# Where the first pair's row terms come from in the opening of a two-layer graph attention kernel, and the order of the work around it

## The chip, the cores and the metric

The kernel runs on one core of a Trainium2 chip. The metric is the device time of one execution in microseconds (us), and the number that counts is the median of several runs. The engines are PE (TensorE, matrix products; PEld is its loading of the stationary operand), DVE (VectorE), ACT (ScalarE), POOL (GpSimd) and SP (SyncE, which here issues the DMAs). Each engine works through a queue of its own in order; semaphores let one wait for another.

## The reference

Two layers over the same graph of 4096 nodes with 256 features: first a network of two graph attention (GAT) steps, then a transformer block whose attention is masked by the same adjacency matrix. Only the first GAT step matters here.

```python
def _gat_layer(x, adj_mat, W, a):            # H = 8 heads, O = 32
    Wh = jnp.einsum('nd,hdo->hno', x, W)
    src = jnp.einsum('hno,ho->hn', Wh, a[:, :O])
    dst = jnp.einsum('hno,ho->hn', Wh, a[:, O:])
    e = jax.nn.leaky_relu(src[:, :, None] + dst[:, None, :], LRELU_SLOPE)
    e = jnp.where(adj_mat[None, :, :] > 0, e, NEG_INF)
    alpha = jax.nn.softmax(e, axis=-1)
    out = jnp.einsum('hnm,hmo->hno', alpha, Wh)
    return jnp.transpose(out, (1, 0, 2)).reshape(N, -1)

h = jax.nn.elu(_gat_layer(x, adj_mat, W1, a1)) + x
out = jax.nn.elu(_gat_layer(h, adj_mat, W2, a2)) + h     # then the transformer
```

`adj` is a 4096 x 4096 matrix of int32.

## The kernel before

**How attention is computed.** exp(leaky_relu(src + dst)) is one of two products of a row factor and a column factor, according to the sign of src + dst. So the kernel builds no exponentials of pairs. For each tile of 128 columns it keeps values that are already multiplied by the two column factors (`vst`, as two fp16 halves), and one-byte matrices that say for each pair whether it is an edge (`mask`) and whether its sum lies on the upper side (`t8`). PE multiplies them (L1462) and adds up in six PSUM banks.

**Groups.** The work of both GAT steps is a list of 256 groups `(l, nb, p, g)`: step, block of 1024 rows, pair of heads, and quarter of 512 columns ("quarter" below means one of these eight pieces, as the change's name does). Eight groups make up one pair of heads for one block. For group i the list `compare(i)` makes `t8`: for each of four column tiles k and two heads j it compares the row terms `s_b` with the column's term `negd` (on DVE as a tensor_scalar, L1124, or on ACT as a Sign, L1122) and then ands the result with the mask on DVE (L1137). `s_b` holds the row terms of a pair of heads, repeated in all 128 partitions; `s_fetch` (L1090) reads it from `s_d` in memory, two DMAs of 512 KB.

**What else the first groups carry.** Quarters are prepared by `preparation(l, q, ...)`: 512 rows of x are transposed on PE (`features`, L991, copied by ACT, L1000); for each of four tiles PE makes the values and terms (`values_out`, L1005, f32), ACT takes exponentials and copies the terms (L1018 to L1020), DVE takes a maximum (L1023) and multiplies by the factors (L1036, L1045) into `prod`; `split` writes the first fp16 half on ACT (L1051) or DVE (L1053) and the second on POOL (L1054). `prod` lies in `ev_broad` for quarter 0 and in `g_prod`, with two buffers, for quarter 1. At last `term_rows` turns a quarter's row terms on PE (L1059), copies them on ACT into `g_sr`, which has one buffer (L1065), and writes them to `s_d` with four small DMAs (L1068).

The adjacency matrix is loaded in units of 256 rows by 512 columns (L858, 512 KB each, buffers `g_adj`, of which there are three; the first eight units have five places elsewhere as well). A unit is clipped to one byte by DVE (`mask_clip`, L867), which also asks for the next load; it is turned on PE (L892) and put into the mask by ACT (L898), and every second one is stored to memory. Four units make the mask of one quarter.

**Order.** In `begin` (L1288) the queues of PE, ACT, DVE and SP follow the written order; after it those of PE, ACT and DVE do, and the steps of preparation, compares, turns and clips are put between the products of each group by due times (`side`). Group i carries `compare(i + 2)`, so `begin` makes `compare(0)` and `compare(1)`. It also prepares quarters 0 and 1 and clips and turns the eight units of their masks; group 0 starts on quarter 2, whose units are in `turns[0]`, the list `ahead`. A few small loads of later code may be put between the DMAs of `begin`.

Written order of `begin` before: loads; features of both quarters; the weights' terms (`weights_steps`); values of quarter 0, with two clips; its term rows; values of quarter 1 with the splits of both and two more clips; its term rows; `s_fetch`; four turns with four clips; `compare(0)`; four turns with the four clips of `ahead`; `compare(1)`.

Of the kernel before, what the change touches and what calls it, by code (L numbers as in the profile page):

```python
# [8 lines left out]
F32 = mybir.dt.float32  # L9
# [13 lines left out]
P = 128  # L23
# [728 lines left out]
def graph_attention(  # L752
# [27 lines left out]
    nc = tc.nc  # L780
    N = adj.shape[0]
    H, D, O = weights[0][0].shape
    DC = D // P
# [4 lines left out]
    W = BT * P  # L788
# [26 lines left out]
    def turn_bank(shape, dtype):  # L815
        return ps.tile(shape, dtype, name="turn", tag="turn", bufs=2)

    spare = []

    def spare_bank():  # L820

        spare.append(0)
        return ps.tile([P, 512], F32, name=f"bank{(len(spare) - 1) % 6}")

# [148 lines left out]
    def rows_ahead(l, q, width=D):  # L975
        if q < NG:
            r = coming_rows[l, q] = rows_p.tile([P, G, D], F32, name="g_rows")
            rows[l].load(r[:, :, :width], G * q, slice(0, width))

    def preparation(l, q, bank, first=False):  # L980
# [32 lines left out]
        def values_in(t):  # L1013
            at = G * q + t
            pv = held.pop(("v", t))
            big = some.tile([P, 2, H], F32, name="g_big", bufs=4)
            for i, scale in enumerate((-1.0, -LRELU)):
                nc.scalar.activation(big[:, i, :], pv[:, D + H : D + 2 * H], AF.Exp, scale=scale)  # L1018
            nc.scalar.activation(L.r[:, at, :], pv[:, D : D + H], AF.Exp, scale=LRELU - 1.0)
            nc.scalar.copy(  # L1020
                L.terms[:, :, at, :], pv[:, D : D + 2 * H].rearrange("p (k h) -> p k h", k=2)
            )
            nc.vector.tensor_reduce(  # L1023
                L.tops[:, at : at + 1], pv[:, :D], AX.X, ALU.max, apply_absolute_value=True
            )

            if l == 0 and q != 1:
                if t == 0:
                    held["prods"] = ep.tile([P, G, H, 2, V1], F32, name="ev_broad")
                prod = held[t] = held["prods"][:, t]  # L1030
            elif l > 0 and t % 2 == 0:
                prod = held[t] = rows_p.tile([P, H, 2, V1], F32, name="g_adj", bufs=3)
            else:
                prod = held[t] = some.tile([P, H, 2, V1], F32, name="g_prod")
            by_head = big.rearrange("p i h -> p h i").unsqueeze(3)
            nc.vector.tensor_tensor(  # L1036
                prod[:, :, :, :O],
                pv[:, :D].rearrange("p (h o) -> p h o", o=O).unsqueeze(2).to_broadcast([P, H, 2, O]),
                by_head.to_broadcast([P, H, 2, O]),
                op=ALU.mult,  # L1040
            )
            if l > 0:
                nc.scalar.mul(prod[:, :, :, O:], by_head, UP)
            else:
                nc.vector.tensor_scalar(prod[:, :, :, O:], by_head, UP, None, op0=ALU.mult)  # L1045
# [41 lines left out]
    def take(n):  # L1087
        return [step for _ in range(min(n, len(later))) for step in later.pop(0)]

    def s_fetch(l, nb, p):  # L1090
        s_b = s_p.tile([P, 2, W], F32, name="s_b")
        first, n = STARTS[l][nb] * P, TILES[l][nb] * P
        for j in range(2):
            row = s_d[l][2 * p + j : 2 * p + j + 1, first : first + n]
            nc.sync.dma_start(s_b[:, j, :n], spread(row, [[0, P], [1, n]]))
        return s_b
# [6 lines left out]
    def compare(i):  # L1103

        l, nb, p, g = groups[i]
        L, s_b = layers[l], s_of[l, nb, p]
        t8 = s8[i] = t_p.tile([P, 2, NW, G, HB], F8, name="t8")
        more = (7, 11, 15, 23, 27, 31)
        if l > 0 or (nb + 1 == len(TILES[l]) and p + 1 < H // 2):
            more = (3, 7, 11, 15, 19, 23, 27)  # L1110
        if apart(i):
            u8[i] = [rows_p.tile([P, NW, G, HB], F8, name="g_adj", bufs=3) for j in range(2)]

        def step(k):
            mt = g * G + k
            for j in range(2):
                to = t8[:, j, :, k, :]
                s = s_b[:, j, :].rearrange("p (w n) -> p w n", n=HB)
                negd = L.negd[:, mt, 2 * p + j : 2 * p + j + 1]

                if (j == 1 or mt in more) and not (i == 0 and k == 0):
                    nc.scalar.activation(to.bitcast(I8), s, AF.Sign, bias=negd, scale=-1.0)  # L1122
                else:
                    nc.vector.tensor_scalar(  # L1124
                        to, s, negd, -1.0, op0=ALU.is_ge, op1=ALU.mult, saturate=False
                    )

        def mask():
            both = t8.rearrange("p j w g n -> p j (w g n)").bitcast(I32)
            m32 = masks[l, nb][g].rearrange("p w g n -> p (w g n)").bitcast(I32)  # L1130
            for j, u in enumerate(u8.get(i, ())):
                nc.vector.scalar_tensor_tensor(
                    u.rearrange("p w g n -> p (w g n)").bitcast(I32),
                    t8[:, j].rearrange("p w g n -> p (w g n)").bitcast(I32),
                    -1, m32, op0=ALU.bitwise_xor, op1=ALU.bitwise_and,
                )
            nc.vector.scalar_tensor_tensor(  # L1137
                both, m32.unsqueeze(1).to_broadcast(list(both.shape)), SIGNS, both,
                op0=ALU.bitwise_or, op1=ALU.bitwise_and,
            )  # L1140

        return [lambda k=k: step(k) for k in range(G)] + [mask]

    def pair_end(l, nb, p, ev):
# [127 lines left out]
    def load_ahead(n):  # L1272
        for _ in range(min(n, len(coming))):
            mask_load(*coming.pop(0))
# [13 lines left out]
    def begin():  # L1288
# [15 lines left out]
        def clip(k):  # L1304
            mask_clip(*units[k], load=False)
# [4 lines left out]
        def both(use):  # L1310
            use[0]()
            use[1]()

        (f_0, v_0, part_0, row_0), (f_1, v_1, part_1, row_1) = (
            preparation(0, q, spare_bank, True) for q in range(2)
        )
        for use in f_0 + f_1:
            both(use)
        for step in weights_steps(0):
            step()  # L1320
        for use in v_0[:2]:
            both(use)
        for k in range(2):
            clip(k)
            both(v_0[2 + k])
        both(row_0)
        for k in range(4):
            both(v_1[k])
            part_0[k]()
            if k < 2:  # L1330
                clip(2 + k)
            if k > 1:
                part_1[k - 2]()
        both(row_1)
        s_of[0, 0, 0] = s_fetch(0, 0, 0)
        rows_ahead(0, 2)
        for k in range(4):
            turn(k)
            if k < 2:
                part_1[2 + k]()  # L1340
            clip(4 + k)
        load_ahead(3)
        ahead = turns[0]
        for step in compare(0):
            step()
        for k in range(4, len(units)):
            turn(k)
            mask_clip(*ahead[k - 4])
        for step in compare(1):
            step()  # L1350

    ev = acc = None
    ordered = {mybir.EngineType.PE, mybir.EngineType.Activation, mybir.EngineType.DVE}
# [821 lines left out]
```

## Time and profile before

| | us |
|---|---|
| median of 3 runs | 3158.15 |
| lowest and highest | 3156.18, 3162.9 |
| the profiled execution's own time | 3161.47 |
| its span | 3159.7 |
| PE busy | 3084.4 (98%) |
| DVE busy | 2786.5 (88%) |
| ACT busy | 2682.1 (85%) |
| POOL busy | 1196.6 (38%) |

The opening, in stretches of 10 us (busy time of each engine):

| stretch | PE | DVE | ACT | granted PE clock | GB/s |
|---|---|---|---|---|---|
| 0 to 10 | 1.85 | 4.16 | 2.18 | 1.00 | 204 |
| 10 to 20 | 9.49 | 7.31 | 6.22 | 1.00 | 383 |
| 20 to 30 | 2.77 | 8.51 | 5.50 | 0.77 | 116 |
| 40 to 50 | 6.76 | 6.05 | 7.62 | 0.88 | 282 |
| 50 to 60 | 8.18 | 9.64 | 6.23 | 0.83 | 265 |
| 70 to 80 | 9.48 | 9.48 | 8.17 | 1.00 | 266 |
| 100 to 110 | 9.63 | 9.49 | 7.93 | 1.00 | 200 |
| 120 to 130 | 8.55 | 8.87 | 8.21 | 1.00 | 120 |

A line of the timeline reads: start in us, duration in us, engine, line of the code, operation, what it writes and reads, shapes, how many instructions are merged, and in brackets how long the engine was idle before and what ended that. "bank" and "turn" are PSUM banks, "t" is `t8`, "adj" a clipped unit. A line of the stretches reads: from and to, length, then busy time and instructions of PE, PEld, DVE, ACT and POOL, the granted clock, the DMA share and GB/s. The clock is recorded from 11.7 us on; the 1.00 before that is not a record.

### The profile page before, as it was taken

How to read it: one execution, taken by the hardware profiler on the slowest of the kernel's cores; microseconds unless marked ns; L12 is line 12 of the kernel's file. 1: busy time of each engine (PE TensorE's matmuls, PEld its weight loads, DVE VectorE, ACT ScalarE, POOL GpSimd, SP SyncE). 2: the span in 40 equal slices, each digit the busy share in tenths (PEclk: the TensorE clock that was granted, in tenths of full speed). 3: DMA queues.
4: the chain of work that ended last, by engine and by line, in shares of the span. 5: the costliest groups of instructions: out<-in, count | busy, mean ns of one | idle time of the engine just before them, and what ended most of it. 6: DMA issues, size and time to landing. Idle time of an engine off the chain costs nothing. (4 is left out here: it accounts for less than half of the span.)

```text
span 3159.7 us, 138934 instructions
## 1 busy us (share of the span) xinstructions
PE 3084.4 (98%) x63976; PEld 2715.3 (86%) x63976; DVE 2786.5 (88%) x3140; ACT 2682.1 (85%) x3228; POOL 1196.6 (38%) x538
## 2 busy tenths in 40 slices
PE   6999999999999999999998999999999999999998
PEld 5899999999889999999975888888878888877766
DVE  7999999999889999999976999999999999998221
ACT  6899999999899999999965888888888888886232
POOL 3300000000320000000003988898988888997110
PEclk8999999999999999999999999999999999999999
DMA  7666554420311213121145010101011010121210
GB/s 259 220 201 197 166 190 149 151 86 23 112 44 39 79 56 96 42 67 38 46 127 158 14 41 21 34 21 34 28 27 39 18 49 8 48 61 56 70 34 22
DMA packets 212034, 250.33 MB, mean 79 GB/s; under 512 B 88241, under 2 KB 132785, under 8 KB 211441
## 3 DMA queue, kind: packets, MB, share of 16 engines
q1 hardware_dynamic: 211440, 241.36, 24.9%
q8 instruction: 502, 8.22, 1.1%
q14 instruction: 92, 0.75, 0.1%
HBM read 198.84 MB, written 42.47 MB: 76 GB/s over the span
## 5 line engine op out<-in xcount | busy, mean ns | idle before, releaser
L1462 PE MATMUL bank<-vst,t 128*128 128x132 f16 x16384 | 1457.3, 220 | 9.7 <-DVE t L1137 9.5
L1946 POOL TENSOR_TENSOR u_both<-u_e 128x1024 f32<-128x1024 f32 x448 | 1049.7, 2385 | 902.8 <-DMA u_k<-half_d 782.8
L1462 PE MATMUL bank<-vst,mask 128*128 128x132 f16 (+1 forms) x10516 | 1372.4, 206 | 0.0
L1122 ACT ACTIVATE t<-s_b,g_terms 128x1024 int8<-128x1024 f32 x1234 | 1320.8, 1162 | 24.3 <-PE bank L1462 18.9
L1462 PEld LDWEIGHTS <-t 128*128 128x128 fp8e4 x16384 | 1186.4, 96 | 22.9 <-DVE t L1137 12.5
L1828 DVE SCALAR_TENSOR_TENSOR u_e<-u_mask,u_ps 128x1024 f32<-128x1024 uint8 x1024 | 1165.9, 1220 | 23.7 <-ACT u_ps L1826 20.6
L1826 ACT ACTIVATE u_ps<-u_ps 128x1024 f32<-128x1024 f32 x1024 | 1030.0, 1008 | 147.4 <-PE u_ps L1819 49.4
L1462 PEld LDWEIGHTS <-mask 128*128 128x128 fp8e4 x10516 | 920.7, 98 | 0.0
L1137 DVE SCALAR_TENSOR_TENSOR t<-mask,t 128x2048 int32<-128x2048 int32 x256 | 588.5, 2299 | 74.8 <-ACT t L1122 66.5
L1819 PE MATMUL u_ps<-u_q,u_k 128*32 128x512 f16 x8192 | 642.6, 383 | 11.0 <-issue 7.3
L1837 PE MATMUL u_av<-u_e,u_v 128*32 128x128 f32 x16384 | 605.7, 273 | 2.6 <-issue 2.6
L1837 PEld LDWEIGHTS u_av<-u_e,u_v 128*32 128x32 f32 x16384 | 492.0, 110 | 131.5 <-issue 5.2
L1124 DVE TENSOR_SCALAR t<-s_b,g_terms 128x1024 fp8e4<-128x1024 f32 x814 | 591.0, 758 | 2.4 <-DMA s_b<-s_d 2.4
L1054 POOL TENSOR_TENSOR vst<-g_adj,vst 128x528 f16<-128x528 f32 x16 | 19.8, 1239 | 727.2 <-ACT g_big L1018 682.7
L1837 PE MATMUL u_dn<-u_both,u_ones 128*32 128x128 f32 x7168 | 281.9, 273 | 1.6 <-issue 1.6
L1819 PEld LDWEIGHTS <-u_k 128*32 128x32 f16 x8192 | 231.4, 95 | 58.6 <-issue 17.9
L1837 PEld LDWEIGHTS u_dn<-u_both,u_ones 128*32 128x32 f32 x7168 | 213.7, 110 | 41.9 <-issue 2.1
L2041 ACT ACTIVATE u_hid<-misc,n_b 128x512 f32<-128x512 f32 x64 | 43.9, 687 | 140.2 <-PE misc L2034 140.1
L2054 PE MATMUL misc<-u_k,u_hid 128*128 128x256 f32 x512 | 111.8, 379 | 0.0
L2034 PE MATMUL misc<-ln_cols,u_k 128*128 128x512 f32 x256 | 111.3, 592 | 0.5 <-ACT ln_cols L1558 0.5
L2054 PEld LDWEIGHTS misc<-u_k,u_hid 128*128 128x128 f32 x512 | 96.7, 190 | 13.3 <-issue 0.5
L2034 PEld LDWEIGHTS misc<-ln_cols,u_k 128*128 128x128 f32 x256 | 48.6, 190 | 58.5 <-issue 56.9
(171 smaller groups left out, 1808.9 us busy)
## 6 DMA issues: line engine op xcount, KB each, us to landing
g_adj<-in_adj_dram SPq DMA_DIRECT2D x123, 512.0 KB
s_b<-s_d SPq DMA_DIRECT2D x64, 512.0 KB
mask<-mask SPq DMA_DIRECT2D x128, 256.0 KB
u_mask<-mask SPq DMA_DIRECT2D x32, 512.0 KB
mask<-stage SPq DMA_DIRECT2D x48, 256.0 KB
half_d<-u_halves SPq DMA_DIRECT2D x32, 256.0 KB
u_q<-half_d SPq DMA_DIRECT2D x32, 256.0 KB
rows<-e_x SPq DMA_DIRECT2D x31, 256.0 KB
```

Of the source, the lines that this page charges most:

```text
L1122: nc.scalar.activation(to.bitcast(I8), s, AF.Sign, bias=negd, scale=-1.0)
L1124: nc.vector.tensor_scalar(to, s, negd, -1.0, op0=ALU.is_ge, op1=ALU.mult, saturate=False)
L1137: nc.vector.scalar_tensor_tensor(both, m32.unsqueeze(1).to_broadcast(list(both.shape)), SIGNS, both, op0=ALU.bitwise_or, op1=ALU.bitwise_and,)
L1462: nc.tensor.matmul(to, left, right, start=k not in opened, stop=last)
L1819: nc.tensor.matmul(ps[r * O : (r + 1) * O, j, :], k_st[c][:, 2 * u + j, at : at + O], q_st[:, h, :], start=True, stop=True,)
L1826: nc.scalar.activation(ps, ps, AF.Exp, scale=SCALE)
L1828: nc.vector.scalar_tensor_tensor(e, mask, 0.0, ps, op0=ALU.not_equal, op1=ALU.mult)
L1837: nc.tensor.matmul(to[j * O : (j + 1) * O, at], lefts[j], es[j // 2][:, j % 2, at], start=first and part == 0, stop=last and part == PARTS ...
L1946: nc.gpsimd.tensor_tensor(both, es_of[i - 1][u], es_of[i][u], op=ALU.add)
L2034: nc.tensor.matmul(ph, w1_sb[:, k, f * P : (f + 1) * P], hn[:, k, :], start=(k == 0), stop=(k == DC - 1),)
L2041: nc.scalar.activation(hid[:, f, :], ph, AF.Gelu_apprx_tanh, bias=norms.sb["b1"][:, f : f + 1])
L2054: nc.tensor.matmul(po[:, :D], hid[:, f, at : at + P], w2_sb[:, f, :], start=(f == 0), stop=(f == FC - 1),)
```

## The change

The change rewrites the order of `begin` and takes the first pair's row terms for block 0 from PE instead of from memory.

- `s_spread(q, j, bank)` multiplies the features of quarter q by one column of the weights, head j's row term, repeated 128 times as the stationary operand. So all 128 partitions of a bank hold that head's row terms, and ACT copies them into `s_b`. Four calls (two heads, two quarters) fill `s_b` for the first pair; `s_fetch(0, 0, 0)` goes. The term rows are still written to `s_d` for the later pairs, at the end of `begin`.
- Twelve f32 products of the identity with itself are put ahead of the features, in a bank of their own (`bank5`), and read by nobody.
- The values of quarter 1 are made after `compare(0)`; the four clips of `ahead` come after `compare(1)`; the rows of quarter 2 and three loads of adjacency are asked for earlier; turns 4 to 7 and both term rows come behind quarter 1's values.
- `banks_of(order)` names the PSUM bank of each step in place of a round of six; term rows use a "turn" bank.
- For quarters 0 and 1 ACT writes the small part of `prod` (L1045 before).
- `compare(0)` returns its steps head by head, and for groups 0 and 1 the tiles k = 0 and 1 of the second head are compared on DVE (before: only k = 0 of group 0).

```diff
-    spare = []
-
-    def spare_bank():
-
-        spare.append(0)
-        return ps.tile([P, 512], F32, name=f"bank{(len(spare) - 1) % 6}")
+    def banks_of(order):
+
+        left = list(order)
+
+        def bank():
+            k = left.pop(0)
+            if k is None:
+                return turn_bank([P, 512], F32)
+            return ps.tile([P, 512], F32, name=f"bank{k}")
+
+        return bank
...
-            if l > 0:
+            if first or l > 0:
                 nc.scalar.mul(prod[:, :, :, O:], by_head, UP)
...
+    def s_spread(q, j, bank):
+
+        L = layers[0]
+        pt = bank()
+        for c in range(DC):
+            nc.tensor.matmul(
+                pt,
+                L.w_ext[:, c, D + j : D + j + 1].to_broadcast([P, P]),
+                L.ft[q][:, c, :],
+                start=(c == 0),
+                stop=(c == DC - 1),
+            )
+        nc.scalar.copy(s_of[0, 0, 0][:, j, q * HB : (q + 1) * HB], pt)
...
-        def step(k):
+        def step(k, heads=range(2)):
             mt = g * G + k
-            for j in range(2):
+            for j in heads:
...
-                if (j == 1 or mt in more) and not (i == 0 and k == 0):
+                if (j == 1 or mt in more) and not (i < 2 and k < 2):
...
+        if i == 0:
+            return [lambda k=k, j=j: step(k, (j,)) for j in range(2) for k in range(G)] + [mask]
...
-            preparation(0, q, spare_bank, True) for q in range(2)
+            preparation(0, q, banks_of(order), True)
+            for q, order in ((0, (0, 1, 4, 5, 0, 1, None)), (1, (2, 3, 4, 5, 2, 3, None)))
         )
+        warm = ps.tile([P, 512], F32, name="bank5")
+        for _ in range(12):
+            nc.tensor.matmul(warm[:, :P], ident_f, ident_f, start=True, stop=True)
         for use in f_0 + f_1:
             both(use)
         for step in weights_steps(0):
             step()
-        for use in v_0[:2]:
-            both(use)
-        for k in range(2):
-            clip(k)
-            both(v_0[2 + k])
-        both(row_0)
+        rows_ahead(0, 2)
+        clip(0)
         for k in range(4):
-            both(v_1[k])
-            part_0[k]()
-            if k < 2:
-                clip(2 + k)
-            if k > 1:
-                part_1[k - 2]()
-        both(row_1)
-        s_of[0, 0, 0] = s_fetch(0, 0, 0)
-        rows_ahead(0, 2)
+            both(v_0[k])
+            if k > 0:
+                part_0[k - 1]()
+                clip(k)
+        part_0[3]()
+        clip(4)
+        s_of[0, 0, 0] = s_p.tile([P, 2, W], F32, name="s_b")
+        s_bank = banks_of((2, 3, 0, 1))
+        for j in range(2):
+            for q in range(2):
+                s_spread(q, j, s_bank)
+        load_ahead(3)
+        ahead = turns[0]
+        comparing = compare(0)
+        for step in comparing[:G]:
+            step()
         for k in range(4):
             turn(k)
-            if k < 2:
-                part_1[2 + k]()
-            clip(4 + k)
-        load_ahead(3)
-        ahead = turns[0]
-        for step in compare(0):
+        clip(5)
+        for step in comparing[G:]:
             step()
-        for k in range(4, len(units)):
+        for use in v_1:
+            use[0]()
+        for k in range(6, 8):
+            clip(k)
+        for k in range(4):
+            v_1[k][1]()
+            if k > 0:
+                part_1[k - 1]()
+        part_1[3]()
+        for k in range(4, 8):
             turn(k)
-            mask_clip(*ahead[k - 4])
+        both(row_0)
+        both(row_1)
         for step in compare(1):
             step()
+        for u in ahead:
+            mask_clip(*u)
```

## The prediction

> **What bounds the kernel now.** I read four views of the execution before: the page, the stretches of ten microseconds, the timeline engine by engine from 0 to 140 us, and the waits. The page says that TensorE is busy for nearly the whole span; the chain that ended last lies in the transformer and does not reach back to the opening. So the question is only how long the opening takes and what passes its delay on.
>
> ```profile
> PEclk8999999999999999999999999999999999999999
> ...
> 30.00:40.00 10.00, 1.83 (x15) 1.57 (x16) 7.12 (x9) 6.18 (x8) 0.00 (x0) 0.50 0.89 299
> ...
> 60.00:70.00 10.00, 8.96 (x107) 7.62 (x105) 9.48 (x14) 8.02 (x24) 4.59 (x3) 1.00 0.76 244
> ...
> 130.00:140.00 10.00, 10.00 (x193) 10.00 (x191) 9.81 (x17) 10.00 (x15) 2.58 (x1) 1.00 0.70 250
> ```
>
> From 130 us on PE is busy in every microsecond; before that it is not. Between 30 and 40 us it works 1.83 of 10 us, at half clock (0.50). The timeline says what it waited for:
>
> ```profile
> 26.71 0.83 SPq L1095 DMA_DIRECT2D s_b<-s_d  x2
> ...
> 33.63 3.23 ACT L1122 ACTIVATE t<-s_b,g_terms 128x1024 int8<-128x1024 f32 x3 [4.82 <-DMA s_b<-s_d]
> 33.63 2.74 DVE L1124 TENSOR_SCALAR t<-s_b,g_terms 128x1024 fp8e4<-128x1024 f32 x4 [2.14 <-DMA s_b<-s_d]
> 36.89 2.29 DVE L1137 SCALAR_TENSOR_TENSOR t<-mask,t 128x2048 int32<-128x2048 int32 x1 [0.52 <-ACT t L1122]
> 39.24 0.40 PE L1462 MATMUL bank<-vst,t 128*128 128x132 f16 x2 [0.78 <-DVE t L1137]
> ...
> 44.94 0.70 DVE L867 TENSOR_SCALAR adj<-g_adj 128x1024 fp8e4<-128x1024 int32 x1 [3.72 <-DMA g_adj<-in_adj_dram]
> ...
> 47.73 2.29 DVE L1137 SCALAR_TENSOR_TENSOR t<-mask,t 128x2048 int32<-128x2048 int32 x1
> ...
> 50.54 0.42 DVE L1023 TENSOR_REDUCE g_tops<-turn 128x1 f32<-128x256 f32 x1
> 51.61 0.40 PE L892 MATMUL turn<-g_ident_h,adj 128*128 128x128 f16 x4 [3.07 <-DVE ev_broad L1036]
> 61.04 2.29 DVE L1137 SCALAR_TENSOR_TENSOR t<-mask,t 128x2048 int32<-128x2048 int32 x1 [0.52 <-ACT t L1122]
> 74.90 2.29 DVE L1137 SCALAR_TENSOR_TENSOR t<-mask,t 128x2048 int32<-128x2048 int32 x1 [0.52 <-ACT t L1122]
> ```
>
> The terms come back from memory at 33.63, so the first group starts at 39.24. But the start is not what is passed on. Group 0 halts at 48.5 until DVE reaches the third quarter's values at 50.54 (PE's 3.07 us wait), since DVE's queue still holds the opening's tail: the second compare's mask (47.73) and a clip that waited 3.72 us for its adjacency tile. From there every group takes the same time: L1137 stands at 47.73, then 61.04, 74.90, 102.69, 116.55, 130.42, 13.86 us apart, DVE 95 to 100% busy, and after 130 PE is full. Nothing there has slack, so **the end moves by as much as DVE's first values of group 0 (50.54) move**. That is my yardstick, not the start at 39.24.
>
> **The change, part by part.** Times "after" are worked out queue by queue, each in its written order, with pitches (start to start) read from the timeline: a values step 0.34 + 0.60 us on DVE (L1023, L1036), a clip 0.61, a compare 0.67, a mask 2.2, a Sign on ACT 1.07 (3.23 for three), a turn's copy on ACT 0.5.
>
> *Warm matmuls.* Twelve f32 products of 128 columns. The trace has none; L1005's halves of 272 columns take 0.24 us each at clock 1.00, so by columns 24 halves take 2.7 us, twice that at half clock. PE is idle until 8.15 (rows landing) and the identity is made by 1.41: 6.7 us of cover, cost nothing. The sixteen first transposes take 0.24 us each; a block of four took 1.06 at clock 0.50 (39.89) and 0.60 at 1.00 (60.03), so they gain up to 1.6 us. The trace's landings put the quarters' rows at 8.0 and 9.5, which leaves 1.1: the values start at 10.4 instead of 11.52. Bounds 0 and 1.6. The Trainium skill (TensorE: Matmul & The Clock Gate, Part 1: The HAM clock gate) says the same, half rate until about 3.4 us of activity, but also that one idle window takes it back; were the gap between the warm matmuls and the rows such a window, its sum would be 0 of gain.
>
> *First quarter's values with clips 0 to 4.* 4 × 0.94 + 5 × 0.61 = 6.8 us of DVE from 10.9 (landing of the first adjacency tile; one more each 1.36 us): done 18.1. ACT takes over L1045 (0.23 us each, as L1043 does in layer 1).
>
> *Spread by PE.* Eight f32 products of 512 columns. The page's L2034 row has 256 records in 111.3 us for 128 such products, 0.87 each: 7.0 us, from 14.3 to 21.3. Four copies like L1000 (0.59). Head 0's terms are there at 18.7, head 1's at 21.9: **the round trip that ended at 33.63 is gone**. Head 0 compares on DVE to 21.4, clip 5, two of head 1 to 23.4; ACT makes four turns and two Signs until 26.1; mask 26.2 to 28.5, against 39.18: 10.7 us earlier. One of head 1's compares (k=1) moves from ACT to DVE, inside the wait for those Signs.
>
> *Second quarter's values.* DVE: clips 6 and 7 (to 29.6), then 3.76 us of values plus two waits for POOL, since g_prod has two buffers. Such waits were 0.71 and 0.78; POOL's subtraction takes 1.14 to 1.67, I take 1.35, so 0.75 each: done 35.6. ACT's last split ends 36.3.
>
> *The tail, where the gain goes.* Turns 4 to 7 now stand on ACT behind all of that: 36.3 to 38.6. Then term_rows, whose g_sr has one buffer. The first copy is at 38.6 to 38.9; its four writes take 1.4 us to issue (16.61 in the trace: 1.37 for four). The second copy must wait until they have landed. Before, 6.5 us lay between the two copies (16.33, 22.79); now nothing does. The price isn't in the trace: at least 0 behind the issue, at most 2.15 (24.56, last write issued, to 26.71, the fetch that reads them). I take 1.3. So ACT stands until 41.7, and behind it in its queue are three Signs of compare(1): 42.0 to 45.1. DVE ends its five compares at 39.0, **stands idle for 6.2 us**, and masks until 47.4. The Trainium skill (DMA: Bandwidth & Descriptors, Anatomy of one DMA) puts a fixed 2.0 us on a DMA, most of it the write receipt; by that the wait would be 0.7 longer.
>
> *SP's queue.* The two 512 KB fetches of s_b go. The rows of quarter 2 and three adjacency loads are issued at 11 to 17 us instead of 27.6 to 32.2; SP waits there for clips 0 to 2, and what is queued behind, the first store of turned masks, is due only at 22.4: nothing. The eight term writes move from 16.6 and 23.1 to 38.9 and 42.0; their next reader is the fetch at 54.88: nothing either. Without that cover the second set's 1.4 us would delay the loads behind it.
>
> *Late clips.* The four clips ahead stood before that mask; they are now last. Their first three tiles land early (the buffers are free after clip 2, at 17 us). The fourth needs the buffer that the first clip frees at 48.0. Issue to use of such a load: 39.82 to 44.94, 5.1 us; across an idle queue at least the 1.36 of the transfer. I take 4.6: landed at 52.6, clipped by 53.3. Group 0's own first clip needs the next load, 1.36 behind: 54.0 to 54.6. Then the values that stood at 50.54: 54.6. Between 26 and 48 us nearly no adjacency is loaded. PE starts group 0 at 39.1 (its queue holds turns 4 to 7 and both term_rows before it), as early as before, and stalls inside it instead. The two DVE compares added to compare(1) lie in the 6.2 us wait; were that gone, they cost 1.3.
>
> **Sum:** 54.6 − 50.54 = +4.1 us. This execution took 3161.47 us (span 3159.7), which gives 3165.6; against the median of the runs, 3158.15, it gives **3162.2**, +0.13%. Bounds. Down: no wait for the g_sr writes −2.6 (the 1.37 of issue too), POOL at 1.14 −0.5, load −0.6: +0.4. Up: no gain from warming +1.1, writes 2.15 +0.9, POOL 1.67 +0.7, load 5.1 +0.5, clips lengthened beside POOL as at 27.07 (1.29 for two) +1.0, four small loads of other code in SP's queue (0.47 each, as at 24.61 to 26.54) +1.9: +10.2.
>
> **Rivals.**
> *Slower: the warm matmuls come too late.* PE's queue also holds the two checks (L833, L840), and L840 needs g_ident_h, made at 9.09. Should the warm matmuls be put behind it, the transposes start at 9.1 + 4.3 = 13.4 and all shifts by some 5 us: 3162.2 + 5 = 3167. It decides from a shift of 2.2 us. For it: these two are not in the hand-written order. Against: before, they stood behind the first transposes (9.68).
> *Faster: DVE never stands.* Its work from the first clip is in place early; if the waits of 0.6, 2.8, 1.5 and 6.2 us all fall away, 3162.2 − 11.1 = 3151. For it: the mask 10.7 us earlier. Against: each wait is a written order.
> *No gain and no loss:* the row copy doesn't wait, ACT ends 2.6 us sooner: 3162.2 − 2.6 = 3159.6.
> *It doesn't do what it says:* the clock was up anyway; then +1.1, inside the forecast's bounds.
>
> **How the numbers follow.** A measurement of this kernel can tell about 0.2%, 6.3 us, from no change. Forecast (late tail) 0.56, its own range +0.4 to +10.2 (3158.5 to 3168.4); above +6.3 lie 4 of its 10, so 0.22 slower, 0.34 same. Slow warm matmuls 0.19, all slower (+9.1). Faster rival 0.15, all faster. No wait 0.10, same. Slower 0.41, same 0.44, faster 0.15. The range leaves most of the faster rival out and adds the runs' own ±3 at the top: 3153 to 3171.
>
> **What would show it.** Right: L1137 first near 26 and second near 45; ACT idle some 2.8 us before L1065; a DVE wait of 3 to 4 us for g_adj near 49; L1023 on "turn" first near 54 to 55; the rest 13.86 apart. Warm: the first L991 block at half its time. Wrong: if that L1023 stands before 48, or if the later groups keep another distance, the yardstick falls; if the first L991 starts after 9, the slower rival holds.

## The result, and the profile after

| | before | after |
|---|---|---|
| median of 7 runs, us | 3158.15 | 3168.86 |
| lowest and highest | 3155.12, 3162.9 | 3166.81, 3172.24 |
| the profiled execution's own time | 3161.47 | 3168.92 |
| its span | 3159.7 | 3167.1 |

The ratio after to before is 1.0033, with an interval of 1.0023 to 1.0042: the changed kernel is slower by 7.3 to 13.3 us, more than the 0.2% from which the prediction counted a change as measurable. 3162.2 was forecast, in a range of 3153 to 3171. So the time lies in the range, but 6.7 us above the forecast.

Line numbers moved with the change. The maximum L1023 is now L1028, the product with the factors L1036 is L1041, the copy of the term rows L1065 is L1070, the Sign L1122 is L1141, the compare L1124 is L1143, the mask L1137 is L1156, the clip L867 is L872 and the load L858 is L863; on PE the transposes L991 are L996, the checks L833 and L840 are L838 and L845, and the values L1005 are L1010. L1100 is the spread, L1107 copies a spread bank into `s_b`, L1341 is a warm product.

First, TensorE's opening in the timeline of the kernel before, then in that of the changed kernel (start, duration, engine, line, what is written and read, how many, and in brackets the idle time before and what ended it):

```profile
8.15 1.94 PE L991 MATMUL bank<-ident,g_rows 128*128 128x128 f32 x8 [8.15 <-DMA g_rows<-in_x_dram]
...
9.96 0.27 PE L840 MATMUL turn<-g_ident_h,g_bits 128*128 128x128 f16 x1
10.02 1.85 PE L991 MATMUL bank<-ident,g_rows 128*128 128x128 f32 x8
11.71 3.83 PE L1005 MATMUL bank<-g_w_ext,g_ft 128*128 128x272 f32 x16
```

```profile
1.46 2.08 PE L1341 MATMUL bank<-ident 128*128 128x128 f32 x8 [1.46 <-POOL ident masks.py:199]
3.33 0.21 PE L838 MATMUL turn<-g_tiny,g_once 128*128 128x2 f16 x1
9.21 0.27 PE L845 MATMUL turn<-g_ident_h,g_bits 128*128 128x128 f16 x1 [5.67 <-DVE g_ident_h L811]
9.28 3.44 PE L1341 MATMUL bank<-ident 128*128 128x128 f32 x16
12.55 1.91 PE L996 MATMUL bank<-ident,g_rows 128*128 128x128 f32 x16
14.30 3.83 PE L1010 MATMUL bank<-g_w_ext,g_ft 128*128 128x272 f32 x16
17.97 7.03 PE L1100 MATMUL bank<-g_ft,g_w_ext 128*128 128x512 f32 x16
```

An f32 product is recorded as two halves (a transpose as one). So only four of the twelve warm products (x8) ran early. Then PE took the two checks in its order, and L845 waited 5.67 us for `g_ident_h`. The other eight (x16) came behind it, and the first transposes, which started at 8.15 before, start at 12.55. They do run at twice the speed (1.91 us for sixteen, against 1.94 for eight before), so of 4.4 us lost, 2.6 are left at the first values: 14.30 instead of 11.71. The spread takes the 7.0 us foreseen.

Next the tail, from the same timeline: ACT, DVE, and SP's queue of DMA issues.

```profile
41.78 0.25 ACT L1070 COPY g_sr<-turn 32x128 f32<-32x128 f32 x1
44.71 0.25 ACT L1070 COPY g_sr<-turn 32x128 f32<-32x128 f32 x1 [2.67 <-DMA s_d<-g_sr]
44.87 3.22 ACT L1141 ACTIVATE t<-s_b,g_terms 128x1024 int8<-128x1024 f32 x3
...
29.78 2.29 DVE L1156 SCALAR_TENSOR_TENSOR t<-mask,t 128x2048 int32<-128x2048 int32 x1 [1.04 <-ACT t L1141]
...
38.73 5.17 DVE L1143 TENSOR_SCALAR t<-s_b,g_terms 128x1024 fp8e4<-128x1024 f32 x5
48.12 2.29 DVE L1156 SCALAR_TENSOR_TENSOR t<-mask,t 128x2048 int32<-128x2048 int32 x1 [4.22 <-ACT t L1141]
50.33 1.90 DVE L872 TENSOR_SCALAR adj<-g_adj 128x1024 fp8e4<-128x1024 int32 x3
56.64 0.70 DVE L872 TENSOR_SCALAR adj<-g_adj 128x1024 fp8e4<-128x1024 int32 x1 [4.41 <-DMA g_adj<-in_adj_dram]
57.96 0.70 DVE L872 TENSOR_SCALAR adj<-g_adj 128x1024 fp8e4<-128x1024 int32 x1 [0.62 <-DMA g_adj<-in_adj_dram]
58.57 0.42 DVE L1028 TENSOR_REDUCE g_tops<-turn 128x1 f32<-128x256 f32 x1
...
68.88 2.29 DVE L1156 SCALAR_TENSOR_TENSOR t<-mask,t 128x2048 int32<-128x2048 int32 x1 [0.52 <-ACT t L1141]
82.75 2.29 DVE L1156 SCALAR_TENSOR_TENSOR t<-mask,t 128x2048 int32<-128x2048 int32 x1 [0.52 <-ACT t L1141]
...
46.36 0.41 SPq L743 DMA_DIRECT2D g_rows<-in_x_dram  x1
47.41 0.81 SPq L1114 DMA_DIRECT2D s_b<-s_d  x2
51.05 8.18 SPq L863 DMA_DIRECT2D g_adj<-in_adj_dram  x5
```

The first mask stands at 29.78 instead of 36.89: the round trip is gone and 7 us are won there. At the second mask the gain is lost (48.12 instead of 47.73): the second row copy waits 2.67 us for the writes of the first, the Signs stand behind it, and DVE waits 4.22 us for them. Then come the clips; the fourth waits 4.41 us for a load issued at 51.05, and the first values of group 0 stand at 58.57 instead of 50.54. That is **+8.0 us at the yardstick**. From there the distances are those of before: 10.31 to the next mask (before 10.50), then 13.87 (13.86).

The stretches of the changed kernel (from and to, length, busy time and instructions of PE, PEld, DVE, ACT and POOL, granted clock, DMA share, GB/s) show where it pays:

```profile
30.00:40.00 10.00, 1.22 (x12) 0.93 (x11) 8.55 (x13) 4.28 (x23) 3.35 (x3) 0.81 0.24 30
...
50.00:60.00 10.00, 6.80 (x44) 5.47 (x45) 4.97 (x10) 2.50 (x10) 0.00 (x0) 0.67 0.81 276
```

The memory has next to nothing to do from 30 to 40 us (30 GB/s, 299 before) and has to catch up from 50 on, while DVE's busy time falls to 4.97 us from 50 to 60 (9.64 before).

### The profile page after: what moved, and what is told of

The parts are those of the page before. It is cut to its first block, busy times and chain, and to the rows that moved or that the text cites. A ratio compares the mean times of both kernels' runs of the same rounds, so it can differ in the third digit from the quotient of the medians.

```text
span 3167.1 us, 139011 instructions
## 1 busy us (share of the span) xinstructions
PE 3096.4 (98%) x64016; PEld 2726.4 (86%) x64016; DVE 2787.8 (88%) x3135; ACT 2679.5 (85%) x3237; POOL 1196.5 (38%) x538
## 4 chain that ended last, share of the span: by engine, by line
PE 48%; ACT 2%; DVE 2%; issue 1%; DMA 0%; DVEq 0%; ACTq 0%
PE u_ps L1855 15%; PE u_av L1873 14%; PE u_dn L1873 8%; PE misc L2090 3%; PE misc L2070 3%; ACT t L1141 2%; PE misc L1793 2%; PE misc L2031 1%; PE misc L1812 1%; DVE t L1143 1%; DVE t L1156 1%; PE misc L1591 0%; ACT ev_broad L1508 0%; DVE u_e L1864 0%; DVE g_adj L1151 0%
## 5 line engine op out<-in xcount | busy, mean ns | idle before, releaser
L1141 ACT ACTIVATE t<-s_b,g_terms 128x1024 int8<-128x1024 f32 x1231 | 1316.0, 1154 | 20.1 <-PE bank L1498 19.5
L1156 DVE SCALAR_TENSOR_TENSOR t<-mask,t 128x2048 int32<-128x2048 int32 x256 | 588.2, 2298 | 79.5 <-ACT t L1141 71.5
L1143 DVE TENSOR_SCALAR t<-s_b,g_terms 128x1024 fp8e4<-128x1024 f32 x817 | 593.8, 758 | 0.2 <-ACT s_b L1107 0.2
L2090 PEld LDWEIGHTS misc<-u_k,u_hid 128*128 128x128 f32 x512 | 96.7, 190 | 13.3 <-issue 0.5
```

What stands on the lines that cost most here:

```text
L1143: nc.vector.tensor_scalar(to, s, negd, -1.0, op0=ALU.is_ge, op1=ALU.mult, saturate=False)
L1156: nc.vector.scalar_tensor_tensor(both, m32.unsqueeze(1).to_broadcast(list(both.shape)), SIGNS, both, op0=ALU.bitwise_or, op1=ALU.bitwise_and,)
L2090: nc.tensor.matmul(po[:, :D], hid[:, f, at : at + P], w2_sb[:, f, :], start=(f == 0), stop=(f == FC - 1),)
```

## The experiments

The theory: the loss has three parts in a row, namely the eight warm products behind the check, the row copy with its one buffer, and the late fourth clip. Each can be taken away alone. The rivals: the parts are hidden behind each other, so that one alone gives nothing; or the spread is itself the loss. All marks below are from the profile of one execution; the ratio is to the kernel before, of all runs. PE's first values are the first L1010 (L1005 in kernels built on the one before); the transformer's first product is where its `u_ps` starts.

| kernel | PE's first values | second mask | first values of group 0 | transformer's first product | median | ratio, interval |
|---|---|---|---|---|---|---|
| before | 11.71 | 47.73 | 50.54 | 1700.6 | 3158.15 | |
| before, second profile | 11.74 | 46.93 | 49.74 | 1698.8 | | |
| after | 14.30 | 48.12 | 58.57 | 1708.0 | 3168.86 | 1.0033, 1.0023 to 1.0042 |
| e1 no warm products | 11.60 | 46.47 | 56.29 | 1705.5 | 3167.35 | 1.0028, 1.0019 to 1.0037 |
| e2 two row buffers | 14.48 | 45.88 | 55.03 | 1704.5 | 3165.68 | 1.0024, 1.0015 to 1.0033 |
| e3 clips earlier | 15.46 | 50.33 | 54.77 | 1704.4 | 3162.16 | 1.0011, 1.0002 to 1.0020 |
| e4 all three | 11.42 | 43.59 | 46.41 | 1695.5 | 3156.43 | 0.9995, 0.9986 to 1.0004 |
| e6 before, and warm products | 15.77 | 50.54 | 53.35 | 1702.7 | 3160.29 | 1.0006, 0.9997 to 1.0016 |
| e7 before, and spread | 11.82 | 45.59 | 48.40 | 1697.9 | 3158.90 | 1.0002, 0.9993 to 1.0011 |
| e8 four warm products | 12.71 | 47.27 | 58.31 | 1708.6 | 3164.85 | 1.0022, 1.0012 to 1.0031 |
| e9 all three, again | 11.70 | 44.01 | 46.83 | 1696.0 | 3157.03 | 0.9999, 0.9990 to 1.0008 |
| e10 all three, Signs earlier | 11.71 | 42.95 | 45.92 | 1695.3 | 3157.74 | 1.0000, 0.9991 to 1.0009 |

### The changed kernel without the warm products (e1)

```diff
-        warm = ps.tile([P, 512], F32, name="bank5")
-        for _ in range(12):
-            nc.tensor.matmul(warm[:, :P], ident_f, ident_f, start=True, stop=True)
```

> The changed kernel without its twelve warm products. In the changed kernel's trace the check of the bits (L845) lies between the fourth and the fifth of them, waits for g_ident_h at 9.2 us, and the features start at 12.55 instead of 8.15; the values at 14.30 instead of 11.52. Theory (three delays add up on DVE's queue: late features, the wait on the row copy, late clips; the end moves with DVE's first L1028 on a turn bank): features back at 8.15, values at 11.5, that L1028 at 55.8 instead of 58.57, time 2.8 us below the changed kernel's, still some 5 to 8 above before. Rival 1 (the warm products alone made it slower): all of the loss goes, L1028 at 50.5 and the time of before. Rival 2 (they help by the clock, the order behind them is what costs): time not lower than the changed kernel's.

PE's opening in its timeline:

```profile
8.02 1.94 PE L996 MATMUL bank<-ident,g_rows 128*128 128x128 f32 x8 [8.02 <-DMA g_rows<-in_x_dram]
9.76 0.21 PE L838 MATMUL turn<-g_tiny,g_once 128*128 128x2 f16 x1
9.83 0.27 PE L845 MATMUL turn<-g_ident_h,g_bits 128*128 128x128 f16 x1
9.89 1.92 PE L996 MATMUL bank<-ident,g_rows 128*128 128x128 f32 x8
11.60 4.60 PE L1010 MATMUL bank<-g_w_ext,g_ft 128*128 128x272 f32 x15
```

The load of the fourth clip, in SP's queue, and the clip, on DVE:

```profile
49.40 7.55 SPq L863 DMA_DIRECT2D g_adj<-in_adj_dram  x5
...
54.27 0.70 DVE L872 TENSOR_SCALAR adj<-g_adj 128x1024 fp8e4<-128x1024 int32 x1 [3.70 <-DMA g_adj<-in_adj_dram]
```

Without the warm products the transposes start at 8.02, the check falls behind the first eight and waits for nothing, and the values start 2.70 us sooner, cold as they are. They then still run partly at half clock (4.60 us for fifteen halves; 3.83 for sixteen in the changed kernel), which gives some of it back: 2.28 us are left at group 0's first values. So the warm products cost about 2.3 us at the mark, read from one profile of each. In the time it is 1.5 us between the medians, and the intervals of the two ratios overlap: shown at the mark, not in the time.

### Two buffers for the row copy (e2)

```diff
-            sr = some.tile([G * H, P], F32, name="g_sr", bufs=1)
+            sr = some.tile([G * H, P], F32, name="g_sr", bufs=2)
```

> The changed kernel with two buffers for g_sr, so that the second quarter's row copy (L1070) needs not wait for the first quarter's four writes to land. Theory: ACT's 2.67 us wait before that copy is gone, the three Signs behind it and DVE's second mask (48.12) come 2.7 us sooner, L1028 at 55.9, time 2.7 us lower. Rival (ACT's lag is hidden, because the loads of adjacency set DVE's start in group 0): the wait goes, but L1028 and the time stay within 1 us.

Its timeline (ACT, DVE, SP's queue):

```profile
42.47 0.25 ACT L1070 COPY g_sr<-turn 32x128 f32<-32x128 f32 x1 [0.23 <-PE turn L1064]
...
45.88 2.29 DVE L1156 SCALAR_TENSOR_TENSOR t<-mask,t 128x2048 int32<-128x2048 int32 x1 [1.79 <-ACT t L1141]
...
53.01 0.70 DVE L872 TENSOR_SCALAR adj<-g_adj 128x1024 fp8e4<-128x1024 int32 x1 [3.02 <-DMA g_adj<-in_adj_dram]
...
46.30 0.34 SPq L1114 DMA_DIRECT2D s_b<-s_d  x1
48.81 6.88 SPq L863 DMA_DIRECT2D g_adj<-in_adj_dram  x5
```

The copy's wait for its writes is gone and the mask comes 2.24 us sooner. The clip gains another 1.4: the load takes 4.20 us from issue to use (48.81 to 53.01), where it took 5.59 (51.05 to 56.64). In the changed kernel rows and two fetches of `s_b` for a later pair, 512 KB each, stand right ahead of the loads in SP's queue; here it is one fetch. That the transfers ahead are what lengthens the load was not tried by itself, and they can explain a part at most: with the same two fetches ahead as in the changed kernel the load took 4.87 us in e1 (49.40 to 54.27). At group 0's first values 3.54 us are won. In the time it is 3.2 us between the medians, and the intervals of the two ratios overlap.

### The clips ahead of group 0 moved forward (e3)

```diff
             if k > 0:
                 part_1[k - 1]()
+            if k < 3:
+                mask_clip(*ahead[k])
...
-        for step in compare(1):
+        comparing = compare(1)
+        for step in comparing[:-1]:
             step()
-        for u in ahead:
-            mask_clip(*u)
+        mask_clip(*ahead[3])
+        comparing[-1]()
```

> The changed kernel with the clips of group 2's quarter moved forward: three of them between the second quarter's values, the fourth ahead of compare(1)'s mask. Theory: the waits for g_adj behind the mask (4.41 and 0.62 us) and three clips go, the loads are asked for near 34 to 38 us; the mask itself stays near 48.1 to 48.6 (ACT sets it); L1028 at 51.5, about 7 us sooner, and the time 7 us lower, near 3162. Rival (loads are late anyway, DMA is the bound): the wait moves to another clip, L1028 gains less than 3.

Its timeline (ACT, DVE):

```profile
46.92 0.25 ACT L1070 COPY g_sr<-turn 32x128 f32<-32x128 f32 x1 [2.96 <-DMA s_d<-g_sr]
...
50.33 2.29 DVE L1156 SCALAR_TENSOR_TENSOR t<-mask,t 128x2048 int32<-128x2048 int32 x1 [4.38 <-ACT t L1141]
52.54 0.69 DVE L872 TENSOR_SCALAR adj<-g_adj 128x1024 fp8e4<-128x1024 int32 x1
54.77 0.42 DVE L1028 TENSOR_REDUCE g_tops<-turn 128x1 f32<-128x256 f32 x1 [1.53 <-ACT g_terms L1025]
```

No clip waits for its tile any more, but only 3.80 of the 5.0 us of load waits come out at the mark, where 7 were expected. Two things stood in the way. The Signs, late behind the row copy, now hold the mask (50.33) and then, on ACT, the exponentials of the third quarter: the values wait 1.53 us for `g_terms`. And in this execution PE's clock rose later (the sixteen transposes took 3.07 us, not 1.91), so that the values started at 15.46 and not at 14.30, which delays all that follows. The time went down by 6.7 us between the medians; the ratios' intervals (1.0002 to 1.0020, 1.0023 to 1.0042) do not meet. Of the single edits to the changed kernel it is the only one whose interval is clear of the changed kernel's.

### All three edits together (e4, and again as e9)

The three diffs above in one kernel.

> The three together: no warm products, two buffers for g_sr, clips forward. Theory: the gains add, 2.8 + 2.7 + 7 = 12.5 us: L1028 near 46, time near 3156.4, some 2 us below before. Rival (one hides behind another: with the clips forward, the mask waits on ACT, whose start is set by DVE's values): less than 9 us, time at or above before's.

> The variant with all three edits once more (no warm products, two buffers for g_sr, clips forward), to narrow its ratio to before. Theory: L1028 on a turn bank again at 46 to 47, some 3.5 to 4.5 us ahead of before's, the transformer's first product (1695.5) ahead by as much, time 1 to 4 us below before. Rival: 46.41 was a lucky landing of loads and the time is that of before.

From the timeline of the first of the two (ACT, DVE):

```profile
40.17 0.25 ACT L1070 COPY g_sr<-turn 32x128 f32<-32x128 f32 x1 [0.24 <-PE turn L1064]
...
43.59 2.29 DVE L1156 SCALAR_TENSOR_TENSOR t<-mask,t 128x2048 int32<-128x2048 int32 x1 [1.67 <-ACT t L1141]
45.80 0.69 DVE L872 TENSOR_SCALAR adj<-g_adj 128x1024 fp8e4<-128x1024 int32 x1
46.41 0.42 DVE L1028 TENSOR_REDUCE g_tops<-turn 128x1 f32<-128x256 f32 x1
```

Group 0's first values come at 46.41, which is 12.16 us sooner than in the changed kernel, where the three single edits give 2.28 + 3.54 + 3.80 = 9.62. Up to 1.2 of the 2.5 us between them may be the late clock of e3 (values at 15.46, not 14.30); the rest fits waits that hid one behind another, which no run separates. The whole loss at the mark is in these three parts, and the spread is not the loss. In the time the kernel is 12.4 us better than the changed one and equal to the one before: 0.9995 (0.9986 to 1.0004), again 0.9999 (0.9990 to 1.0008). By the marks it should be some 3 to 5 us better than before; it was not measured to be (see below).

### The kernel before with the warm products alone (e6)

```diff
+        warm = ps.tile([P, 512], F32, name="bank5")
+        for _ in range(12):
+            nc.tensor.matmul(warm[:, :P], ident_f, ident_f, start=True, stop=True)
         for use in f_0 + f_1:
```

> The kernel before with the twelve warm products ahead of the features and nothing else. Theory: the check of the bits splits them as in the changed kernel, the features start at 12.5 instead of 8.15 and the values 2.8 us later; DVE's L1023 on a turn bank moves by 2.3 to 2.8 us, as taking them out of the changed kernel moved it by 2.28; time 2 to 3 us above before. Rival (warming pays: the features run at full clock and PE has slack in the opening): no later than before.

PE's opening in its timeline, and DVE's first values of group 0:

```profile
9.27 3.73 PE L1319 MATMUL bank<-ident 128*128 128x128 f32 x16
12.79 3.14 PE L991 MATMUL bank<-ident,g_rows 128*128 128x128 f32 x16
15.77 3.83 PE L1005 MATMUL bank<-g_w_ext,g_ft 128*128 128x272 f32 x16
...
53.35 0.42 DVE L1023 TENSOR_REDUCE g_tops<-turn 128x1 f32<-128x256 f32 x1
```

The same happens in the old order: eight products behind the check, transposes at 12.79. Here they hardly warmed: the sixteen transposes take 3.14 us, most of them at half clock. The mark moves by +2.8 us against the first profile of the kernel before, +3.6 against the second. The ratio, 1.0006 (0.9997 to 1.0016), does not tell this from nothing.

### The kernel before with the spread alone (e7)

```diff
+        s_of[0, 0, 0] = s_p.tile([P, 2, W], F32, name="s_b")
+        for j in range(2):
+            for q in range(2):
+                s_spread(q, j, spare_bank)
         both(row_1)
-        s_of[0, 0, 0] = s_fetch(0, 0, 0)
```

`s_spread` is that of the change.

> The kernel before with the four spread products in place of the fetch of s_b, behind the second quarter's values and ahead of its term rows; nothing else moves. Theory: the compares no longer wait for memory (33.63), but PE's 7 us stand ahead of the turns; compare(0) runs from about 30 us, its mask ends near 36 instead of 39.2, and the four clips and the load behind it follow 3 us sooner: L1023 near 47.5, time 3 us below before. Rival (the round trip was hidden, DVE is bound by its own work): less than 1 us.

ACT and DVE in its timeline (the mask is L1151 here):

```profile
27.52 0.59 ACT L1102 COPY s_b<-bank 128x512 f32<-128x512 f32 x1 [1.13 <-PE bank L1095]
...
29.83 5.18 DVE L1138 TENSOR_SCALAR t<-s_b,g_terms 128x1024 fp8e4<-128x1024 f32 x5
35.12 2.29 DVE L1151 SCALAR_TENSOR_TENSOR t<-mask,t 128x2048 int32<-128x2048 int32 x1
...
48.40 0.42 DVE L1023 TENSOR_REDUCE g_tops<-turn 128x1 f32<-128x256 f32 x1
```

The terms are complete in `s_b` at 28.1 (27.52 + 0.59), 5.5 us ahead of the 33.63 at which DVE had the last of them before. But then the clips take DVE until 29.83, and the five compares behind them fall beside POOL's subtractions (29.34 to 32.47 in the same timeline) and take 5.18 us (two of them 1.64 us each, the other three 0.74); before, the last four took 2.74. Of the 5.5 us 1.8 are left at the mask (35.12, not 36.89) and 1.3 to 2.1 at group 0's first values. The time is 1.0002 (0.9993 to 1.0011): the spread alone is no loss; the 3 us that were expected of it did not show.

### The changed kernel with four warm products (e8)

```diff
-        for _ in range(12):
+        for _ in range(4):
```

> The changed kernel with four warm products instead of twelve, so that all of them lie ahead of the check of the bits. Theory: the features still stand behind that check, which waits for g_ident_h until 9.2, so they start at 9.5, and at half clock, since PE was idle for over 5 us before: values at about 13.3 instead of 14.30, L1028 near 57.6, time 1 us below the changed kernel's and about 1 us above the variant without warm products. Rival (four are enough to raise the clock and the check costs nothing): values at 10.5, L1028 near 55.

Its timeline (PE, DVE):

```profile
9.29 3.62 PE L996 MATMUL bank<-ident,g_rows 128*128 128x128 f32 x16
...
57.70 0.70 DVE L872 TENSOR_SCALAR adj<-g_adj 128x1024 fp8e4<-128x1024 int32 x1 [1.94 <-DMA g_adj<-in_adj_dram]
58.31 0.42 DVE L1028 TENSOR_REDUCE g_tops<-turn 128x1 f32<-128x256 f32 x1
```

Four products all run ahead of the check, and the transposes follow it at 9.29: still 1.3 us later than without any, since they now stand behind L845's wait. The values start at 12.71, 0.6 us sooner than expected. The mark didn't follow: the second mask comes 0.85 us sooner than in the changed kernel, group 0's first values only 0.26, because group 0's own first clip waited 1.94 us for its load here (0.62 in the changed kernel). That is a scatter of 1.3 us in one load's landing; this run settles the place of the check in PE's order and not the price at the mark. Its median lies 4.0 us below the changed kernel's and 2.5 below that of e1, where 1 below and 1 above were expected; the intervals of the three ratios overlap, so the time tells them apart no better.

### All three edits, and two Signs made earlier (e10)

`compare(1)` starts with two compares of its second head on ACT, ahead of the third tile of the second quarter's values; head 0's tile k = 3 goes to DVE in exchange.

```diff
-                if (j == 1 or mt in more) and not (i < 2 and k < 2):
+                if (j == 1 or (mt in more and i != 1)) and not (i == 0 and k < 2):
...
+        if i == 1:
+            pairs = [(0, 1), (1, 1), (0, 0), (1, 0), (2, 0), (2, 1), (3, 0), (3, 1)]
+            return [lambda k=k, j=j: step(k, (j,)) for k, j in pairs] + [mask]
...
+            if k == 1:
+                comparing = compare(1)
+                for step in comparing[:2]:
+                    step()
...
-        comparing = compare(1)
-        for step in comparing[:-1]:
+        for step in comparing[2:-1]:
```

> The same variant, with two of compare(1)'s compares (head 1, tiles 0 and 1) given back to ACT and put where ACT stood idle for 3.72 us before the second quarter's first split, and one (head 0, tile 3) given to DVE. Theory: ACT's last stretch is one Sign shorter (1.07 us) and DVE has one compare less; ACT's feature copies and DVE's second mask come 1.1 us sooner, L1028 near 45.3, time 1 us below the variant without it, 2 to 5 below before. Rival (ACT and PE of group 0 are not what the values wait for): L1028 stays at 46.4.

The second mask comes at 42.95 and group 0's first values at 45.92, 0.5 to 0.9 us ahead of the two profiles without this edit, somewhat less than expected; the time is that of the kernel before (1.0000, 0.9991 to 1.0009).

### The kernel before once more (e5)

> The kernel before, unchanged, profiled once more, to see how far its own opening moves from run to run. Theory: its order is fixed and only the landings of loads vary, so L1023 on a turn bank stays within 1 us of 50.54 and the marks L1137 at 61.04, 74.90 and so on with it; what the runs differ by (3155 to 3163 us) lies elsewhere. Rival: the first profile caught a slow opening, and L1023 now stands some 3 us earlier, which would explain why the measured losses of the changed kernel and its variants are about 3 us above the shifts of the marks.

No edit. Its marks stand 0.8 us (group 0's first values) to 1.8 us (the transformer's first product) ahead of the first profile, and the last `u_ps` product 4.2 us ahead: 2883.8 against 2888.0. The part from the first to the last `u_ps` product alone took 1187.4 us in one and 1185.0 in the other, and between 1184.8 and 1190.2 in all the profiles. So the first profile was not of an opening that was slow by 3 us, the rival here, and the times' distance from the marks (below) is not explained by it. A difference of 2 to 3 us between two single executions' times says nothing. The changed kernel's +8.0 at the mark is +8.8 against this profile.

## Why the prediction was right and wrong

**The yardstick held as far as the transformer.** Group 0's first values moved by 8.0 us (8.8 by the second profile), the transformer's first product by 7.4 (9.2), the time by 7.3 to 13.3. What the opening lost was not made up later, as the prediction said from the full DVE and PE behind it. In all ten profiles of a changed order the transformer's first product moved as far as the mark within 1.0 us. Behind that the one-to-one is loose. By the medians the time is 2.6 to 4.7 us worse than the mark's shift (against the first profile before) in seven kernels, the changed one, e1, e2, e4, e7, e9 and e10, and within 1.3 us of it in e3, e6 and e8; no run says why. Of the prediction's list of masks "13.86 us apart" the first distance is 13.31 (47.73 to 61.04).

**The tail was right in kind and nearly in size.** The round trip went and the gain was lost at the row copy: ACT's wait there is 2.67 us where 2.7 was foreseen (1.4 of issue and 1.3 of landing), and e2 takes it away. The writes were issued by 43.6 and freed the copy by 44.7, some 1.1 us. The Trainium skill (DMA: Bandwidth & Descriptors, Anatomy of one DMA) would have put 2.0 here; its figure is fitted on DMAs issued from GpSimd, these are issued from SP, and for these small writes the trace decides. POOL's waits were 0.53 and not 0.75 each. DVE's wait before the mask is 4.22 and not 6.2, since the five compares, two of them beside POOL's subtractions, took 5.17 us instead of 3.35; that cost nothing, because ACT was later still.

**The step that failed: "cost nothing" for the warm matmuls.** It counted 6.7 us of cover, from the identity's making to the rows' landing, as if all twelve could use it. The two checks stand among them in PE's queue, and L845 holds the rest until 9.21. The values of the first quarter therefore start at 14.30 and not at 10.4, and the mask ends at 50.33 and not at 47.4: **2.9 of the 4.0 us by which the mark missed its forecast (58.57, not 54.6)**. Some 1.6 of the 2.9 are the wait behind the check: without the warm products (e1) the values start at 11.60 and the mask ends at 48.68. The other 1.3 are the gain that was booked for warming and that no run shows: full rate came no earlier with the warm products than without (see the last section). (The 11.52 at which the prediction has the values start before is the load of their weights; the product itself started at 11.71.) The slower rival named this very mechanism, with L840 and the time at which `g_ident_h` is made, at a chance of 0.19; it put the transposes at 13.4 (12.55 measured) and the price at 5 us. The price at the mark is 2.3 (e1) to 3.6 us (e6, against the second profile before). The argument against it, that the checks stood behind the first transposes before, was no argument: the transposes waited for a load until 8.15 then, and the warm products wait only for the identity (1.46), so they are the ones that a check can be put between; why it fell behind the fourth of them no run shows. So the forecast's tail and the rival's cause came true together, a case that had no place among the chances.

**Mis-sized: the load of the fourth clip.** 4.6 us from issue to use were forecast, 5.6 measured: the remaining 1.0 us. The prediction took a queue with nothing just ahead; in fact 1 MB of `s_b` for a later pair and rows of x had been issued before (46.36 to 48.2). How much of the 1.0 us they made is open: with the same transfers ahead the load took 4.87 us in e1 and 4.86 in e8 (50.20 to 55.06), so they explain at most some 0.3 of it (4.9, not 4.6) and what made the other 0.7 no run shows. Those transfers follow the eight term writes, which the change moved to 42.25. The prediction said of these writes that their next reader is due late and that the move costs nothing; the reader itself, brought next to the loads, was left out. The four small loads of other code, which stood in the bounds with 1.9 us, cost nothing: they fell to 29 to 32 us.

**The sum.** Forecast +4.1; measured +8.0 at the mark, of which 3.9 are the two items above. The time's +10.4 (7.3 to 13.3) agrees with 8.0 to 8.8 within what runs differ by. The forecast's own range ended at 3168.4, just below the 3168.86 measured, and the overall range held it only by the 3 us that were added at its top for the scatter of the runs. That the time fell inside is in part luck: the slower rival's cause, which the forecast had set aside, came on top of the forecast's tail.

**What stays open.** With all three edits the opening is 3 to 5 us ahead of the kernel before at group 0's first values and at the transformer's first product, in three profiles (e4, e9, e10); the medians of the three lie 0.1 us above to 1.2 us below the kernel before that ran with them. Each interval by itself allows a gain of 3 to 4 us, and single profiles scatter by as much, so either the gain is there and too small to tell, or the transformer gives a part of it back. No run tells these apart.

## What to carry to other kernels

"The engine is idle then" is cover only for instructions that nothing in the same in-order queue can be put between: look for every other instruction with a wait of its own that is free to fall among the new ones, and ask what stands behind it. When a wait is taken out of an opening, follow the freed engine to the next thing it is late for (here a buffer used twice in a row, then clips whose loads are asked for by the clips themselves), and mend those in the same change; one at a time the three edits gave 9.6 us at the mark, together 12.2. A transfer that moves can take its later reader along, so look at what that reader puts ahead of others in the DMA queue as well.

## What the runs showed of the hardware

- The clock did not rise at a fixed time after the warm products. The same sixteen transposes behind the same twelve products took 1.91 us (after), 2.13 (e2), 3.07 (e3) and 3.14 (e6): from all at full rate to most of them at half. Read from where the distance between products halves, full rate came at about 12.2, 12.9, 14.8 and 15.2 us, which is 3.0 to 6.0 us after PE had become busy without a break (8.94 to 9.22); the clock's first record lies within 0.1 us of each (12.29, 12.95, 14.91, 15.30). Without warm products it came at 11.0 (e4) to 13.9 us (before, second profile), 2.9 to 5.8 us after the first transposes began. So the warm products brought full rate no earlier. The Trainium skill (TensorE: Matmul & The Clock Gate, Part 1: The HAM clock gate) has PE go to full rate after some 3.4 us in a free-running window, with a spread of 0.5 us either way from where in the window the work begins; the spread here is larger.
- The first four warm products, with 5.67 us of idle PE behind them, warmed nothing: in e8 the transposes that follow take 3.62 us, as cold as without any.
- A compare of 128 x 1024 on DVE that began while a subtraction of POOL ran took 1.63 or 1.64 us in four cases (two in the changed kernel, two in e7), one that did not 0.74. Each of the four ended 0.55 us after that subtraction, and the subtractions, 1.14 us when alone, took 1.54 to 1.59 and ended 1.0 us after the DVE instruction that ran when they began: the two engines took turns. So five compares took 5.17 and 5.18 us there; before, four took 2.74 with POOL idle.
- A 512 KB load took 4.2 us (e2), 4.9 (e1 and e8) and 5.6 (after) from issue to use. One fetch of `s_b` had been issued ahead of it in e2, two in the three others, so the spread among those is as large as the step from one fetch to two.
